# A decoder layer on one core: constant products at the start, the first norms by two token tiles, and a moved turn between two batches

## The chip, the core and the metric

The kernel is one program on one core of a Trainium2 chip. The metric is the time of one execution in microseconds (us), measured on the device. The engines are PE (TensorE: matrix products and transposes), DVE (VectorE), ACT (ScalarE), POOL (GpSimd) and SP (SyncE, which issues most of the transfers here). Each engine works through its own list of instructions in order and waits at an instruction until what it needs has been signalled.

## The reference

Input is x of 4 batches x 512 tokens x 512 features. Three stages, each of them added to x:

```python
x = x + attn(layernorm(x), w_norm, W_in, w_conv, dt_bias, A_log, W_h2i, W_out)
x = x + xattn(layernorm(x), ctx_512, ctx_512)
x = x + ffn(layernorm(x), gate_w, expert_bias, shared_*, experts_*)

# attn: a state-space mixer
xn   = x * rsqrt(mean(x * x) + EPS) * w_norm
proj = xn @ W_in.T                   # z, xi, dt, B, C
xi   = silu(depthwise_conv(xi, width 4))
dt   = softplus(dt + dt_bias);  dA = exp(dt * -exp(A_log))
u    = (dt * mean_over_head(xi))[..., None] * B
h    = dA * h + u  (along the tokens);  y = sum(h * C)
out  = ((y @ W_h2i.T) * silu(z)) @ W_out.T + x_in

# xattn: 32 query heads over 8 key heads of size 16, softmax, keys = values = ctx
# ffn: sigmoid router, 2 of 16 experts per token, and one shared expert
```

The mixer is given layernorm(x), and its own residual adds this input again; so the first stage gives x + layernorm(x) + mixer(layernorm(x)).

## The kernel before

All tokens are held in `res` (128 partitions x 16 token tiles x 512 features). A batch is four token tiles (TB = 4). The mixer of a batch is the generator `ssm(b)`; the attention runs in 32 units (4 batches x 8 key heads) of 8 steps; the router, the shared expert and the blocks of the routed experts follow.

The order of instructions on PE, DVE and ACT is the order in which the Python program writes them (`manual_schedule`); POOL's and SP's lists follow the tile framework. Work that follows a product is not written at once but put on a list, `lag`, with one queue for DVE and one for ACT; `lag.step()` writes out what has become due. The generators yield the estimated PE time of a piece of work, or None where they wait for something on that list.

**The start.** `make_identity` lets POOL write `ident`. The first four token tiles of `res` are loaded by four transfers (L69). `ssm_stats(0)` takes the statistics of the four tiles on DVE (L244, L245) into `smv`, then over all four at once: Sqrt on ACT (L262), three small DVE operations (`square`, L249 to L251), Sqrt on ACT (L266), four small DVE operations (`rest`, L254 to L258). The mixer's own root mean square follows from the variance, so both norms are one scale, `srn`. `ssm_normed(b, j)` writes the normed tile `xn` (L100, on DVE for batch 0 and on POOL later) and on POOL turns the tile of `res` into x + layernorm(x) (L280), with `sr` and `st`. `nega` is -exp(A_log) (L988 on ACT, L989 on DVE).

**The turn.** `ssm_turn(b, j)` transposes `xn` on PE into the PSUM tile `ptx` (L294, four 128x128 transposes) and DVE multiplies it by w_norm into `xnT` (L295); then it calls `ssm_normed(b, j + 2)`, since `xn` has two buffers. PSUM tiles of this kind come from a pool of three. When the four tiles are there, `project` (L311) multiplies `xnT` by pieces of W_in: `pd` (dt), `px`, `pz`, `pb`, `pc`, each of four products, which the trace records as eight.

**Between batch 0 and batch 1.** `ssm(0)` runs alone, without attention beside it. At its end, for each token tile, `po` (L456) is W_out's product, DVE adds it to `res` (L463), takes the statistics for the attention's queries (`part`, L87, L88) and then comes the turn of the tile of batch 1. After the fourth tile `power_q` finishes `rstdq` (L76 on ACT, L77 on DVE), and `norm_queries` lets POOL write the normed queries `qp` (L100). Four pieces of `ssm(1)` are then written, two projections `pd` in two halves each, and after them `queries(0, "q")`: PE transposes `qp` into `ptq` (L532) and ACT copies it to `qTq` (L536).

**The attention's steps.** In each step `maxima` runs two products `pm` (L544) whose maxima DVE takes (L550, into `qp`), `weights` runs `pw` (L561) whose exponentials ACT takes (L565), and `fill(step)` puts in a piece of the next batch's mixer. `pm` and `pw` share a pool of two PSUM tiles. In the first unit there are no `pw` yet. `fill` spends a quota of PE time for each step:

```python
        while owed > 0 or last:
            ...
            if us is not None:
                owed -= us
            elif last:
                lag.step(dve=99.0)
            else:
                return
```

so a piece that waits for the list ends the step's filling, except where the batch's work has to be finished.

## Time and profile before

| | us |
|---|---|
| median of 3 runs | 1420.57 |
| lowest, highest | 1419.97, 1430.86 |
| the profiled execution, its time | 1417.93 |
| its span in the trace | 1415.9 |
| PE busy | 1351.2 (95%) |
| DVE busy | 701.1 (50%) |
| ACT busy | 491.5 (35%) |
| POOL busy | 370.8 (26%) |
| mean granted clock of PE (1 is full) | 0.984 |

A busy PE is not PE at its peak: its clock is granted by a throttle, and the trace gives the granted clock for any stretch. A line of the waits says which engine and line waited for whom, for how many us in total, how often, and the longest. A line of the chain gives start, duration and what ran. A line of the timeline gives start, duration, engine, line, operation, output <- inputs, shapes, number of instructions, and in brackets the idle time before it with what ended it. PEld is PE's loading of weights, which can lie beside its products.

### The profile page before, as it was taken

The page shows a single profiled execution, that of the slowest core. Times are in us where ns is not written, and L with a number is a line of the kernel's source. Part 1 is how long each engine was busy: PE and PEld are TensorE (multiplying, and loading weights), DVE is VectorE, ACT ScalarE, POOL GpSimd, SP SyncE. Part 2 cuts the span into 40 slices and gives each one's busy share as a digit, 9 for nine tenths or more (in the row PEclk, how much of TensorE's full clock was granted, in tenths as well). Part 3 has the DMA queues.
Part 4 walks back from the last instruction along what each step waited for, and adds up shares of the span by engine and source line. Part 5 has one row for each costly group of instructions (what it writes and reads, how often), then busy time and mean ns, then how long its engine had stood idle before and what let it go on. Part 6 is the DMA issues. An engine that isn't in the chain of part 4 may idle for free.

```text
span 1415.9 us, 15833 instructions
## 1 busy us (share of the span) xinstructions
PE 1351.2 (95%) x5776; PEld 538.3 (38%) x5776; DVE 701.1 (50%) x1028; ACT 491.5 (35%) x652; POOL 370.8 (26%) x368
## 2 busy tenths in 40 slices
PE   6999999999999999999999999999999999999894
PEld 3444333333333333333333333333333644444442
DVE  4562656554565645456564446455565653332231
ACT  3220434533544353354434345444443111111110
POOL 4023010302111132111112113212100037776675
PEclk9999999999999999999999999999999899999997
DMA  9200000000000000000000200100000186778764
GB/s 352 31 1 0 0 5 5 4 4 7 4 10 8 4 4 7 6 4 11 6 5 19 66 13 12 31 34 28 29 15 23 52 319 124 138 186 213 205 135 49
DMA packets 61502, 76.84 MB, mean 54 GB/s; under 512 B 22640, under 2 KB 34928, under 8 KB 61168
## 3 DMA queue, kind: packets, MB, share of 16 engines
q1 hardware_dynamic: 45104, 53.24, 11.6%
q0 software_dynamic: 15456, 22.03, 9.0%
q8 instruction: 48, 0.79, 0.2%
q10 hardware_dynamic: 864, 0.55, 0.1%
q14 instruction: 30, 0.25, 0.1%
HBM read 96.76 MB, written 19.92 MB: 82 GB/s over the span
## 4 chain that ended last, share of the span: by engine, by line
PE 86%; DVE 6%; DMA 3%; ACT 2%; issue 1%; POOL 0%; POOLq 0%; SPq 0%; DVEq 0%; ACTq 0%
PE pm L544 18%; PE pgb L1400 9%; PE po L456 8%; PE px L311 8%; PE pz L311 8%; PE pav L571 7%; PE pob L1424 4%; PE pw L561 3%; DVE qp L550 3%; DMA out_x<-y,half_i 2%; PE pd L311 2%; PE pb L311 2%; PE pi L444 2%; PE pc L311 2%; PE pg L688 2%; PE ptq L532 1%
## 5 line engine op out<-in xcount | busy, mean ns | idle before, releaser
L550 DVE TENSOR_REDUCE qp<-pm 128x2 f32<-128x1024 f32 x256 | 313.6, 1225 | 352.3 <-PE pw L561 292.6
L565 ACT ACTIVATE ex<-pw 128x1024 f32<-128x1024 f32 x256 | 262.2, 1024 | 387.7 <-PE pw L561 387.6
L544 PE MATMUL pm<-kt,qTq 16*128 16x512 f32 x1024 | 287.8, 640 | 12.3 <-DVE qp L550 10.8
L561 PE MATMUL pw<-qTm,kt 17*128 17x512 f32 x1024 | 289.5, 641 | 5.1 <-ACT ex L565 4.4
L100 POOL TENSOR_SCALAR qp<-res,mvq,rstdq 128x64 f32<-128x64 f32 x128 | 74.3, 600 | 333.5 <-PE ptm L532 299.4
L1400 PE MATMUL pgb<-ring,xT 128*128 x336 | 153.3, 599 | 2.4 <-DVE xT L1394 2.3
L544 PEld LDWEIGHTS pm<-kt,qTq 16*128 16x128 f32 x1024 | 76.4, 183 | 189.7 <-DVE qp L550 92.3
L1433 POOL DMA_INDIRECT out_x<-y,half_i x84 | 131.5, 1565 | 64.1 <-DMA out_x<-y,half_i 39.3
L571 PE MATMUL pav<-ex,va 128*32 128x512 f32 x1024 | 123.1, 598 | 0.0
L311 PE MATMUL px<-xnT,ssm_large 128*128 128x512 f32 x256 | 121.4, 616 | 0.0
L311 PE MATMUL pz<-xnT,ssm_large 128*128 128x512 f32 x256 | 119.3, 602 | 0.4 <-DVE xc L368 0.3
L456 PE MATMUL po<-ssm_large 128*128 128x512 f32 x256 | 118.5, 599 | 0.0
L590 POOL TENSOR_TENSOR res<-res,o 128x256 f32<-128x256 f32 x32 | 26.7, 833 | 325.8 <-DVE o L586 324.2
L561 PEld LDWEIGHTS pw<-qTm,kt 17*128 17x128 f32 x1024 | 76.8, 183 | 28.8 <-ACT qTm L536 15.0
L1400 PEld LDWEIGHTS pgb<-ring,xT 128*128 128x128 f32 x336 | 61.2, 192 | 64.7 <-issue 61.6
L1424 PE MATMUL pob<-ring,aT 128*128 x168 | 79.1, 593 | 0.5 <-ACT aT L1415 0.5
L368 DVE SCALAR_TENSOR_TENSOR xc<-px,wcv,xc 128x511 f32<-128x511 f32 (+2 forms) x96 | 71.7, 746 | 7.8 <-ACT xc L364 5.6
L311 PEld LDWEIGHTS px<-xnT,ssm_large 128*128 128x128 f32 x256 | 47.2, 194 | 64.8 <-issue 63.1
L1407 DVE TENSOR_TENSOR actb<-pgb,sgb 128x256 f32<-128x256 f32 x42 | 17.8, 424 | 107.3 <-ACT sgb L1405 107.2
L311 PEld LDWEIGHTS pz<-xnT,ssm_large 128*128 128x128 f32 x256 | 45.7, 190 | 63.0 <-issue 59.7
L1429 DVE TENSOR_SCALAR y<-pob,wslot 128x512 f32<-128x512 f32 x42 | 31.5, 751 | 70.6 <-DMA out_x<-y,half_i 44.5
L456 PEld LDWEIGHTS po<-ssm_large 128*128 128x128 f32 x256 | 45.4, 190 | 54.5 <-issue 53.0
(214 smaller groups left out, 1318.4 us busy)
## 6 DMA issues: line engine op xcount, KB each, us to landing
ring<-in_experts SPq DMA_DIRECT2D x42, 1536.0 KB
kt<-in_ctx_t SPq DMA_DIRECT2D x128, 32.0 KB
h_d<-hn SPq DMA_DIRECT2D x16, 256.0 KB
out_x<-res SPq DMA_DIRECT2D x16, 256.0 KB
res<-in_x SPq DMA_DIRECT2D x3, 1024.0 KB
ssm_large<-in_w_in SPq DMA_DIRECT2D x2, 1024.0 KB
ssm_large<-in_w_out SPq DMA_DIRECT2D x1, 2048.0 KB
ssm_large<-in_w_in SPq DMA_DIRECT2D x6, 256.0 KB
```

Source lines behind the costliest of these rows:

```text
L100: eng.tensor_scalar(dst, src, mv[:, j, 0:1], rstd[:, j : j + 1], ALU.subtract, ALU.mult)
L311: nc.tensor.matmul(pm, lhsT=win[:, piece, c, :], rhs=xnT[:, c, :], start=(c == 0), stop=(c == DC - 1),)
L368: nc.vector.scalar_tensor_tensor(xc[:, d:], px[:, : L - d], wcv[:, i, KW - 1 - d : KW - d], xc[:, d:], ALU.mult, ALU.add,)
L456: nc.tensor.matmul(po, lhsT=zg[:, i, ts(j, P)], rhs=wout[:, i, :], start=(i == 0), stop=(i == IC - 1),)
L544: nc.tensor.matmul(ps[:, g - g0, :], lhsT=qT[g * SL : g * SL + HD, ts(j, P)], rhs=kts[i % NQ][g * SL : g * SL + HD, :], start=True, stop=True,
L550: nc.vector.tensor_reduce(qps[i % NQ][:, j, g0 : g0 + 2, HD], ps, AX.X, ALU.max, negate=True)
L561: nc.tensor.matmul(ps[:, g - g0, :], lhsT=kts[i % NQ][rows, ts(c, P)], rhs=qT[rows, :], start=True, stop=True,)
L565: nc.scalar.activation(ex, ps, AF.Exp, scale=1.0 / HD**0.5)
L571: nc.tensor.matmul(pav[ts(g, SL), :], lhsT=vas[b % 2][:, c, v, :], rhs=ex[1 - g // 2][:, g % 2, :], start=(c == 0), stop=(c == TB - 1),)
L1400: weigh(k, nc.tensor.matmul(pg, lhsT=xT[:, c, :], rhs=weight(k, c), start=(c == 0), stop=(c == DC - 1),))
L1424: weigh(k, nc.tensor.matmul(po, lhsT=aT[:, f, :], rhs=weight(k, DC + f), start=(f == 0), stop=(f == FC - 1),))
L1433: add = nc.gpsimd.indirect_dma_start(out=out_halves, out_offset=bass.IndirectOffsetOnAxis(ap=half_i[:, h, k : k + 1], axis=0), in_=y[:, ts ...
```

## The change

1. Behind the constants of the start, PE is given 24 products of `ident` with itself into a PSUM tile `awake` that nobody reads.
2. The statistics of batch 0 go by two halves, tiles 0 and 1 (`lo`) and tiles 2 and 3 (`hi`), written out by hand with the normed tiles between them. `rest` is cut in two: `rest` gives `srn`, and `add` gives `st` and `sr`, for which nothing of the turn waits. For batch 0 `add` and POOL's operation on `res` (now in `ssm_added`) come after all four turns.
3. In batch 0's turn the tiles 1 and 3 are evacuated by ACT, in four operations of 128 columns each (Copy with a scale); tiles 0 and 2 stay with DVE.
4. At the end of `ssm(0)` the query statistics `part(j)` come after the turn of the next batch.
5. `queries(0, "q")` is written after two of the four first pieces of `ssm(1)`, that is between the two `pd`.
6. In the steps before step 4, `fill` steps the list on rather than end the step.

```diff
+    awake = bank("awake", (P, P))
+    for _ in range(24):
+        nc.tensor.matmul(awake, lhsT=ident, rhs=ident, start=True, stop=True)
...
-        def square():
-            nc.vector.reciprocal(r, r)
-            nc.vector.tensor_mul(t, r, r)
-            nc.vector.tensor_mul(t, t, mv[:, :, 1])
-        def rest():
-            nc.vector.reciprocal(rn, rn)
-            nc.vector.tensor_mul(rn, rn, r)
-            nc.vector.tensor_mul(t, r, mv[:, :, 0])
-            nc.vector.tensor_scalar_add(r, r, 1.0)
+        def roots(j):
+            nc.scalar.activation(r[:, j], mv[:, j, 1], AF.Sqrt, bias=eps_ln)
+        def square(j):
+            nc.vector.reciprocal(r[:, j], r[:, j])
+            nc.vector.tensor_mul(t[:, j], r[:, j], r[:, j])
+            nc.vector.tensor_mul(t[:, j], t[:, j], mv[:, j, 1])
+        def roots_n(j):
+            nc.scalar.activation(rn[:, j], t[:, j], AF.Sqrt, bias=eps_rms)
+        def rest(j):
+            nc.vector.reciprocal(rn[:, j], rn[:, j])
+            nc.vector.tensor_mul(rn[:, j], rn[:, j], r[:, j])
+        def add(j):
+            nc.vector.tensor_mul(t[:, j], r[:, j], mv[:, j, 0])
+            nc.vector.tensor_scalar_add(r[:, j], r[:, j], 1.0)
+        if b == 0:
+            return part, roots, square, roots_n, rest, add
...
@@ ssm_normed
         normed(nc.vector if b == 0 else nc.gpsimd, xn, r, mv, ms, j)
+        xns[b, j] = xn
+        if b > 0:
+            ssm_added(b, j)
+    def ssm_added(b, j):
+        mv, ms, r1, mr = ssm_of[b]
+        r = res[:, b * TB + j, :]
         nc.gpsimd.tensor_scalar(
             r, r, r1[:, j : j + 1], mr[:, j : j + 1], ALU.mult, ALU.subtract
         )
-        xns[b, j] = xn
@@ ssm_turn
-        nc.vector.tensor_tensor(
-            xnTs[b][:, :, ts(j, P)], pt,
-            wn.unsqueeze(2).to_broadcast([P, DC, P]), ALU.mult,
-        )
-        ssm_normed(b, j + 2)
+        xT = xnTs[b][:, :, ts(j, P)]
+        if b == 0 and j % 2 == 1:
+            for c in range(DC):
+                nc.scalar.activation(xT[:, c], pt[:, c], AF.Copy, scale=wn[:, c : c + 1])
+        else:
+            nc.vector.tensor_tensor(
+                xT, pt, wn.unsqueeze(2).to_broadcast([P, DC, P]), ALU.mult
+            )
+        if b > 0:
+            ssm_normed(b, j + 2)
@@ ssm, start
             for j in range(TB):
                 ssm_turn(b, j)
+                ssm_normed(b, j + 2)
                 yield TR
+            for j in halves:
+                add_norms(j)
+            for j in range(TB):
+                ssm_added(b, j)
@@ ssm, end
             nc.vector.tensor_add(r, po, r)
-            if b == 0:
-                part(j)
             yield 2 * MM
             if b < B - 1:
                 ssm_turn(b + 1, j)
             else:
                 ffn_turn(0, j, nc.gpsimd)
+            if b == 0:
+                part(j)
             yield TR
@@ the program's order
-    for _, _, fn in ssm_stats(0):
-        fn()
-    for j in range(2):
-        ssm_normed(0, j)
+    part, roots, square, roots_n, rest, add_norms = ssm_stats(0)
+    halves = lo, hi = slice(0, 2), slice(2, TB)
+    part(0); part(1)
+    roots(lo); square(lo); roots_n(lo)
+    part(2); part(3)
+    roots(hi); rest(lo); ssm_normed(0, 0)
+    square(hi); roots_n(hi); ssm_normed(0, 1)
+    rest(hi)
     nc.scalar.activation(nega, nega, AF.Exp)
     nc.vector.tensor_scalar_mul(nega, nega, -1.0)
...
-    for _ in range(4):
+    for n in range(4):
+        if n == 2:
+            qT_of = {0: queries(0, "q")}
         us = next(work)
         done += us or 0.0
         lag.step(dve=99.0)
-    qT_of = {0: queries(0, "q")}
@@ fill
-            elif last:
+            elif last or step < TB:
                 lag.step(dve=99.0)
```

More of the change, by code (lines that the diff above doesn't have):

```diff
@@ L245, in part @@
             nc.vector.bn_aggr(out=mv[:, j, :], in_=st)
-        def square():
-            nc.vector.reciprocal(r, r)
-            nc.vector.tensor_mul(t, r, r)
-            nc.vector.tensor_mul(t, t, mv[:, :, 1])
-        def rest():
-            nc.vector.reciprocal(rn, rn)
-            nc.vector.tensor_mul(rn, rn, r)
-            nc.vector.tensor_mul(t, r, mv[:, :, 0])
-            nc.vector.tensor_scalar_add(r, r, 1.0)
+        def roots(j):
[14 more added lines that the diff above has]
+            return part, roots, square, roots_n, rest, add
+        j = slice(0, TB)
         return (
             *[(ENG.DVE, 0.9, lambda j=j: part(j)) for j in range(TB)],
-            (ENG.Activation, 0.3, lambda: nc.scalar.activation(
-                r, mv[:, :, 1], AF.Sqrt, bias=eps_ln
-            )),
-            (ENG.DVE, 0.6, square),
-            (ENG.Activation, 0.3, lambda: nc.scalar.activation(rn, t, AF.Sqrt, bias=eps_rms)),
-            (ENG.DVE, 0.8, rest),
+            (ENG.Activation, 0.3, lambda: roots(j)),
+            (ENG.DVE, 0.6, lambda: square(j)),
+            (ENG.Activation, 0.3, lambda: roots_n(j)),
+            (ENG.DVE, 0.8, lambda: (rest(j), add(j))),
         )
@@ L981, in route_early @@
         yield from until(lagged(ops + share(0, T1)))
-    for _, _, fn in ssm_stats(0):
-        fn()
-    for j in range(2):
-        ssm_normed(0, j)
+    part, roots, square, roots_n, rest, add_norms = ssm_stats(0)
+    halves = lo, hi = slice(0, 2), slice(2, TB)
+    part(0)
+    part(1)
+    roots(lo)
+    square(lo)
+    roots_n(lo)
+    part(2)
+    part(3)
+    roots(hi)
+    rest(lo)
+    ssm_normed(0, 0)
+    square(hi)
+    roots_n(hi)
+    ssm_normed(0, 1)
+    rest(hi)
     nc.scalar.activation(nega, nega, AF.Exp)
```

## The prediction

> **What bounds the kernel now.** I read the page's busy table and its chain first, then the waits of PE, then the chain and the timeline of the two places that the change touches, and last the stretches with their granted clock.

> ```profile
> PE 1351.2 (95%) x5776; PEld 538.3 (38%) x5776; DVE 701.1 (50%) x1028; ACT 491.5 (35%) x652; POOL 370.8 (26%) x368
> ...
> PE 86%; DVE 6%; DMA 3%; ACT 2%; issue 1%; POOL 0%; POOLq 0%; SPq 0%; DVEq 0%; ACTq 0%
> ```

> PE is the bound nearly everywhere: only its idle time and its slow time can be won, 1415.9 - 1351.2 = 65 us of idle in all, and 28 us of that lie after 1100 us, in the last router and the expert blocks, which this change does not touch. The waits of PE (total, times, longest) say where the rest is:

> ```profile
> PE ptx L294 <- DVE xn L100: 12.0, 2, 11.2
> PE pm L544 <- DVE qp L550: 10.8, 23, 1.5
> ...
> PE pd L311 <- DVE xnT L295: 2.7, 2, 1.9
> ...
> PE pm L544 <- ACT qTq L536: 1.5, 1, 1.5
> ```

> Of the first, 11.2 is the start of the program. Of the second only one wait of 1.34 lies at the start of the attention; 6.8 of the 10.8 fall between 700 and 1000 us. The chain of the start (start, us, what):

> ```profile
> 11.21 1.10 PE ptx L294 x4
> ...
> 12.34 0.69 DVE xnT L295
> 13.03 0.85 DVE xn L100
> ...
> 16.19 0.70 DVE xnT L295
> ...
> 16.93 9.12 PE pd L311 x16
> ```

> The first projection starts at 16.93 and takes 9.12; the same projection of the second batch takes 7.15. So 1.97 us go to a slow PE. The timeline between the batches:

> ```profile
> 136.32 0.66 DVE L295 TENSOR_TENSOR xnT<-ptx,wn 128x512 f32<-128x512 f32 x1
> ...
> 137.04 7.13 PE L311 MATMUL pd<-xnT,ssm_large 128*128 128x512 f32 x16 [1.94 <-DVE xnT L295]
> ...
> 146.08 1.13 PE L544 MATMUL pm<-kt,qTq 16*128 16x512 f32 x4 [1.48 <-ACT qTq L536]
> 147.14 5.40 PE L311 MATMUL px<-xnT,ssm_large 128*128 128x512 f32 x8
> ...
> 154.95 1.13 PE L544 MATMUL pm<-kt,qTq 16*128 16x512 f32 x4 [1.34 <-DVE qp L550]
> ```

> Three waits, and a px that takes 5.33 where eight records at the usual 0.43 are 3.44. The stretches (busy of PE, weight loads, DVE, ACT, POOL; then granted clock, DMA share, GB/s) give the reason:

> ```profile
> 143.97:147.38 3.41, 1.93 (x10) 0.90 (x9) 0.84 (x2) 1.79 (x3) 0.00 (x0) 0.98 0.02 5
> 147.38:150.79 3.41, 3.41 (x5) 1.35 (x5) 1.13 (x1) 0.00 (x0) 0.00 (x0) 0.52 0.00 0
> 1103.02:1106.43 3.41, 3.41 (x18) 3.41 (x18) 0.00 (x0) 1.52 (x3) 0.00 (x0) 0.50 0.34 131
> ```

> After a thin stretch of 3.41 us (transposes, a wait, products of 16 rows) the clock is half for the next one. At the start the column shows 1.00, but weight loads take 0.34 us until 20.85 and 0.19 from 21.17 on, the same pair as around 150.7, so I read that as half clock too. 21.1, 147.38, 150.79 and 1099.6 lie on one grid of 3.41 us. The last line: in a stretch full of transposes and products of 16 columns the clock stays at half.

> **The change, part by part.**

> *The 24 constant products.* They wait for ident, which POOL finishes at 1.72 us; nothing else wants PE before 10 us. In the order of instructions they stand ahead of the first transposes. Each is two records. Their price is bounded by ptab (94 columns, 64 records, 7.5 us busy: 0.118 each at full clock) and by the 16-column pl at half clock (eight in 1.73: 0.22). That is 48 x 0.118 = 5.7 to 48 x 0.22 = 10.6 us, so they end between 7.4 and 12.3. With half clock until about 7.4 (two grid lines after their start) it is some 25 records slow and 23 fast, 5.5 + 2.7, end near 10.

> *Norms by two tiles.* DVE's order is now: statistics 0 and 1, three small operations, statistics 2 and 3, two small, xn0, three small, xn1, two small, nega, xnT0, xn2, xn3, xnT2. From the rows: statistics 1 end at 6.52; Sqrt 0.30 to 6.85; three DVE steps of 0.2 to 7.45; statistics 2 and 3 (0.69, 0.18 and 0.66, 0.18) to 9.16; reciprocal and product to 9.45; xn0 to about 10.05, against 11.1 before, so the first transpose can start at 10.15 instead of 11.21. Then the gain is lost again. ACT runs its second pair of roots at 9.2 and 10.6; the Exp table (1.28, row L988) is loaded only then, to 12.2, Exp of nega ends at 12.4, and DVE's nega operation, which stood at 11.48 before, waits for it at 12.44. Behind it on DVE stand xnT0, xn2, xn3, and PE's third and fourth transposes wait for those. So xnT0 ends at 13.2 (13.03 before), xn2 at 13.75, xn3 at 14.25. xn2 takes 0.55 instead of 0.85, because POOL's operation on res (L280, 2.1 to 2.3) no longer runs beside it. Third and fourth transposes at 1.10 (slow): 13.85 to 16.0.

> *ACT evacuates half.* A slice of 128 columns is not in the trace; it lies between 0.20 (nega, two columns) and 0.37 (aT, 256 columns): 0.28. xnT1 is taken after nega, 12.4 to 13.5, hidden. Of xnT3 only the first slice delays pd: 16.05 + 0.3 = 16.4, against 16.93, where DVE needed the whole 0.70. The three later slices lie under pd's records. The four adds (DVE) and POOL's L301 now follow; the sums are wanted at 112 us by L463, nothing waits. At fast transposes (0.55) pd would start at 15.4.

> *Is PE fast when pd starts?* Between the end of the constant products (about 10) and pd (16.4) PE runs only 16 transposes, 4.2 us at most in 6.3. The stretch 143.97 to 147.38 was busy for 1.93 of 3.41 and the clock fell. So I take it that it falls here as well, and that pd pays the 1.97 again. Start: -0.5 us. The bounds: -0.5 - 1.0 - 1.97 = -3.5 if it stays fast; +0.3 if the constant products stay slow to 12.3 and push everything (ptx0 12.3, xn2 14.6, pd 17.25).
> [...]

> *Statistics after the turn.* xnT of the last tile follows its residual add at once: 135.50 instead of 136.32, pd at 136.2 instead of 137.04: -0.85. What is late next: the queries' statistics end at 137.0 (136.40 before), so the root, the reciprocal and POOL's four operations (0.56 each) end at 140.0 instead of 139.4.

> *Queries between the two pd.* ptq now stands behind the first pd, which ends at 136.2 + 3.44 = 139.65: PE waits about 0.4 for POOL. In return ACT copies qTq at 142.5 (behind Abs, the Exp table, Exp) under the second pd, and pm finds it ready: -1.48 + 0.4 = -1.1. The thin stretch is gone (ptq, pd, pm, px follow each other), so px runs at full clock: 5.33 - 3.44 = -1.9.

> *No step ends early before step 4.* Before, fill returned and left pm 1, 2 and 3 back to back; the third waited 1.34 for a reduction (1.23, two buffers). Now px halves (1.72) stand between them. Followed by hand: reductions of pm1, taps (2.31), plus (1.30), a table load, silu, reductions of pm2 and pm3 end at 157.2 and 158.4 on DVE; PE reaches pm4 at 158.6 and pm5 at 163.1, so neither waits. -1.3. Taps and silu that now stand ahead of the reductions are the cover that could go: one step later on DVE costs what pm4 then waits, up to 1.2. Bounds +1.2 and -1.3.

> *The order after that.* PE's order differs up to the last transposes for batch 2 (some 355 us) and is the same from there on. The amount of work is the same; the waits in that stretch are 0.4 now. I take 0, with the bounds in the rivals.

> Sum: -0.5 - 0.85 - 1.1 - 1.9 - 1.3 = -5.65. Against the profiled execution (span 1415.9, time 1417.93) that is 1412.3. The median of the runs shown, 1420.57, lies 2.64 above it; I forecast for the median: 1414.9.

> **The rivals.**
> *A. PE stays fast into pd.* For: the stretch 133.73 to 137.14 had PE busy for 1.48 of 3.41 and kept its clock. Against: half of that was full products, which the new gap has none of. -3.0 more: 1411.9.
> *B. The drop at 147 is not there to be won.* The clock falls only if the thin piece (144.0 to 147.1) fills one interval of the grid. In timed runs the grid may lie otherwise. Then 1.9 is missing: 1416.8.
> *C. The moved order makes PE wait in the attention.* Place: pm and pw between 160 and 355. For: with the mixture of 700 to 1000 us pm waits 13 times, 6.8 us in all, and a pw waited 1.87 where three table loads stood ahead of its Exp. Against: the amount of filler per step is unchanged. If both appear, +8.7: 1423.6. It decides from 5.65 us of waits on.

> **How the numbers follow.** Forecast 0.57, A 0.17, B 0.18, C 0.08. The likeliest is 1414.9. The range takes in A and its bound below (another 3 us for a drop less in the expert stage, where 1099 to 1113 and 1335 to 1338 run at half clock) and reaches to B and the three runs' spread above: 1408.5 to 1421.5. About 1% (14 us) is what a measurement of this kernel can tell from no change, and all four cases lie within it; beyond it only something not seen here would lead: 0.03 each side, 0.94 within.

> **What would show it.** Right: constant products until about 10 us; nega on DVE near 12.4, right after a table load; pd at about 16.4 with weight loads of 0.34 for its first four microseconds; second pd about 0.85 after the last residual add; no wait of pm on qTq; clock 1.00 around 147. Wrong: weight loads of 0.19 from pd's start (A); half clock between 140 and 160 (B); more than 2 us of waits on qp or ex before 355 (C).

## The result, and the profile after

| | before | after |
|---|---|---|
| median of the timed runs, us | 1424.65 | 1416.24 |
| lowest, highest | 1417.47, 1430.86 | 1410.76, 1421.73 |
| the profiled execution, its time | 1417.93 | 1417.91 |
| its span in the trace | 1415.9 | 1415.8 |

The ratio of after to before is 0.9949 with a 95% interval of 0.9935 to 0.9963, that is 5.3 to 9.3 us less, 7.3 in the middle (the two medians differ by 8.4). The forecast was 1414.9 from a gain of 5.65. The two profiled executions take the same time. That is no contradiction, and b2 below shows why; for this reason the steps are compared between marks inside the traces and not by the spans.

The busy table and the chain of the profile after:

```profile
PE 1361.2 (96%) x5824; PEld 545.1 (39%) x5824; DVE 699.6 (49%) x1033; ACT 493.6 (35%) x662; POOL 369.7 (26%) x368
...
PE 83%; DVE 7%; DMA 5%; issue 2%; ACT 2%; POOL 1%; SPq 0%; POOLq 0%; DVEq 0%; ACTq 0%
```

PE is busy for 10 us more: 7.5 are the constant products, which lie in time that was idle before. PE's waits after (total, times, longest):

```profile
PE pm L574 <- DVE qp L580: 9.2, 22, 1.5
...
PE ptx L314 <- DVE xn L100: 3.2, 3, 2.1
```

One wait on `qp` less (1.6 us less in all), the `xnT` wait between the batches 1.01 where it was 1.94, and no line for `qTq` any more. The start in the timeline:

```profile
1.78 7.48 PE L235 MATMUL awake<-ident 128*128 128x128 f32 x48 [1.78 <-POOL hmean L213]
...
10.87 1.28 ACT L1031 ACT_TABLE_LOAD   x1
...
12.40 0.17 DVE L1032 TENSOR_SCALAR nega<-nega 128x2 f32<-128x2 f32 x1 [1.15 <-ACT nega L1031]
...
13.77 1.94 PE L314 MATMUL ptx<-ident,xn 128*128 128x128 f32 x8 [2.09 <-DVE xn L100]
...
16.17 8.70 PE L341 MATMUL pd<-xnT,ssm_large 128*128 128x512 f32 x16 [0.46 <-ACT xnT L318]
```

DVE waits for a table load before `nega`, everything behind it is late, and `pd` is slow (8.70; the second batch's takes 3.70 + 3.60). The stretches (busy of PE, weight loads, DVE, ACT, POOL; granted clock, DMA share, GB/s):

```profile
9.13:12.54 3.41, 1.44 (x10) 0.84 (x8) 2.08 (x12) 2.25 (x6) 0.00 (x0) 1.00 1.02 402
12.54:15.95 3.41, 1.94 (x8) 1.57 (x8) 2.53 (x8) 1.05 (x5) 0.00 (x0) 0.50 1.01 404
...
142.41:145.82 3.41, 3.41 (x11) 1.43 (x11) 1.88 (x2) 1.32 (x2) 0.63 (x2) 1.00 0.00 0
```

The first line is the gap behind the constant products; the clock falls at its end and stays down until 19.36. The last line is the first `pm` and its `px` in the second batch, now at full clock. That place in the timeline:

```profile
134.93 3.70 PE L341 MATMUL pd<-xnT,ssm_large 128*128 128x512 f32 x8 [1.01 <-DVE xnT L320]
138.47 0.60 PE L562 MATMUL ptq<-ident,qp 128*128 128x128 f32 x4
138.91 3.60 PE L341 MATMUL pd<-xnT,ssm_large 128*128 128x512 f32 x8
142.44 1.13 PE L574 MATMUL pm<-kt,qTq 16*128 16x512 f32 x4
143.49 3.70 PE L341 MATMUL px<-xnT,ssm_large 128*128 128x512 f32 x8
147.12 1.13 PE L574 MATMUL pm<-kt,qTq 16*128 16x512 f32 x4
```

Of the stalls of before, the wait on `qTq` and the slow `px` are gone, and the wait before `pd` is 0.93 shorter. The wait of the third `pm` is gone as well, but the row that shows its price comes with j3.

### The profile page after: what moved, and what is told of

The parts are those of the page before. It is cut to its first block, busy times and chain, and to the rows that moved or that the text cites. A ratio compares the mean times of both kernels' runs of the same rounds, so it can differ in the third digit from the quotient of the medians.

```text
span 1415.8 us, 15947 instructions
## 1 busy us (share of the span) xinstructions
PE 1361.2 (96%) x5824; PEld 545.1 (39%) x5824; DVE 699.6 (49%) x1033; ACT 493.6 (35%) x662; POOL 369.7 (26%) x368
## 3 DMA queue, kind: packets, MB, share of 16 engines
HBM read 96.76 MB, written 19.92 MB: 82 GB/s over the span
## 4 chain that ended last, share of the span: by engine, by line
PE 83%; DVE 7%; DMA 5%; issue 2%; ACT 2%; POOL 1%; SPq 0%; POOLq 0%; DVEq 0%; ACTq 0%
PE pm L574 18%; PE po L486 8%; PE pz L341 8%; PE px L341 8%; PE pav L601 8%; PE pgb L1444 7%; PE pob L1468 3%; DMA out_x<-y,half_i 3%; PE pw L591 3%; DVE qp L580 3%; PE pd L341 2%; PE pb L341 2%; PE pi L474 2%; PE pc L341 2%; PE pg L718 2%
## 5 line engine op out<-in xcount | busy, mean ns | idle before, releaser
L100 POOL TENSOR_SCALAR qp<-res,mvq,rstdq 128x64 f32<-128x64 f32 x128 | 73.9, 596 | 335.6 <-PE ptm L562 301.2
L1426 POOL DMA_INDIRECT res<-h_d,row_i x42 | 45.6, 1085 | 74.2 <-DVE half_i L1288 41.9
```

Source lines behind the costliest of these rows:

```text
L100: eng.tensor_scalar(dst, src, mv[:, j, 0:1], rstd[:, j : j + 1], ALU.subtract, ALU.mult)
```

## The experiments

| run | median, us | before beside it | ratio | 95% interval |
|---|---|---|---|---|
| a1_no_awake | 1417.32 | 1422.67 | 0.9961 | 0.9940 to 0.9983 |
| a2_bridge | 1414.03 | 1422.67 | 0.9929 | 0.9904 to 0.9955 |
| a3_nega_late | 1411.71 | 1422.67 | 0.9903 | 0.9870 to 0.9937 |
| a4_old_start | 1418.35 | 1422.67 | 0.9964 | 0.9944 to 0.9984 |
| j1_stats_first | 1414.62 | 1422.42 | 0.9935 | 0.9912 to 0.9958 |
| j2_queries_late | 1418.12 | 1422.42 | 0.9972 | 0.9953 to 0.9992 |
| j3_steps_end | 1415.59 | 1422.42 | 0.9937 | 0.9910 to 0.9964 |
| k1_fill_thin | 1425.72 | 1422.42 | 1.0019 | 0.9994 to 1.0044 |
| a5_bridge_nega | 1411.89 | 1425.48 | 0.9917 | 0.9891 to 0.9943 |
| p2_bridge_thin | 1410.51 | 1425.48 | 0.9895 | 0.9871 to 0.9919 |
| j4_dve_turns | 1415.09 | 1425.48 | 0.9937 | 0.9914 to 0.9960 |
| b2_before_again | 1420.04 (one run) | | | |

The intervals are some 0.005 wide, 7 us, and most single parts are 0.5 to 3 us. So the times alone separate few of these runs; the traces do, since the same mark of PE's order can be read to 0.1 us. (The median of a3, for one, is a little below that of a5, which contains its edit and starts the first `px` 2.9 us earlier.) At the start a trace also has its own shift of some tenths: the first transposes start at 9.74 to 10.19 in the traces with the new start.

### The start: a1, a2, a3, j4

**a1, without the constant products.**

```diff
-    awake = bank("awake", (P, P))
-    for _ in range(24):
-        nc.tensor.matmul(awake, lhsT=ident, rhs=ident, start=True, stop=True)
```

> The changed kernel without the 24 constant products. Theory (the clock has fallen again before the first projection, so the products buy nothing): the first transposes run at 1.1 us a tile instead of 0.55, but DVE waits for nega until 12.4 anyway; pd starts at 16.2 to 16.6 and its first four weight loads or so take 0.34; the time is that of the changed kernel within 1 us, ratio to the kernel before 0.995. Rival (on the average over runs the products do carry the clock into pd): 2 us slower than the changed kernel, ratio 0.9965, with a profile that looks like that of the kernel before at 17 to 26 us.

Measured: `pd` starts at 15.94, takes 8.33, and the first `px` starts at 24.10 (24.71 with the products). The ratio, 0.9961, lies nearer to the rival's 0.9965 than to the theory's 0.995, but its interval holds both. One trace does not decide it either, since the grid of the clock lies elsewhere in each execution (its first line at 0.1 to 3.3 us in the fourteen traces) and the end of the slow time with it. All traces together do: without constant products `pd` takes 8.33 to 9.40, in the mean 8.87 (before, b2, a1, a4, k1); with the 24 products and the gap behind them 8.59 to 9.08, in the mean 8.86 (after, a3, j1 to j4). So the products as they stand buy nothing in `pd`.

**a2, more products in the gaps between the transposes** (`keep(n)` issues n of them, all into a tile of another pool).

```diff
+    keep(24)
...
+                if j == 0:
+                    keep(3)
...
+                keep((1, 8, 0, 2)[j])
```

> The changed kernel with 14 more constant products, set where PE is idle between the first ones and pd: 3 ahead of the first turn, 1 behind it, 8 behind the second, 2 behind the fourth (all write a PSUM tile of the attention's pool, which nobody reads). Theory (it is the thin gap that takes the clock back): granted clock 1.00 from 12 to 20 us, last two transposes 0.55 each, pd starts at about 15.3 with weight loads of 0.19, px starts at 22.4 instead of 24.7, 2.3 us less than the changed kernel, ratio to before 0.9935. Rival (products of 128 columns and transposes are too light to hold the clock, or the grid decides): the clock falls all the same, and the products ahead of the third turn take 0.44 each and delay it by up to 1.5 us: 0 to 1.5 us slower than the changed kernel.

Measured, in PE's timeline:

```profile
15.19 7.13 PE L350 MATMUL pd<-xnT,ssm_large 128*128 128x512 f32 x16
22.16 3.17 PE L350 MATMUL px<-xnT,ssm_large 128*128 128x512 f32 x7
```

The transposes of the last two tiles take 1.11 where they took 1.94, `pd` 7.13 where it took 8.70, and `px` comes 2.55 us earlier. Beside the products in the gaps only the place of the grid differs, and that is not the reason: in the six traces with the open gap (after, a3, j1 to j4) the clock falls at 11.8 to 14.4 us wherever the grid lies, and in the three with filled gaps (a2, a5, p2) it does not fall there and `pd` takes 7.13 each time. The thinnest interval of the gap is busy for 2.74 of 3.41 us here (8.03 to 11.44), where it was 1.44. So the gap behind the 24 products is what loses their effect.

**a3, DVE's nega operation behind the turns.**

```diff
     nc.scalar.activation(nega, nega, AF.Exp)
-    nc.vector.tensor_scalar_mul(nega, nega, -1.0)
...
             for j in range(TB):
                 ssm_added(b, j)
+            nc.vector.tensor_scalar_mul(nega, nega, -1.0)
```

> The changed kernel with DVE's multiplication of nega moved behind the turns and the adds of batch 0 (ACT's Exp stays where it is). Theory (DVE's wait for the Exp table is what takes back the gain of the two-tile norms): xnT0 at 11.3 instead of 12.48, xn2 and xn3 by 13.1, third transposes at 12.6 instead of 13.8, pd at 15.1 instead of 16.17; 1.1 us less than the changed kernel. Rival (ACT is next late: xnT1 behind the table load, or slow transposes set the pace): pd at 15.8 to 16.2, less than 0.4 us gained.

Measured: the first `xnT` starts at 11.02 (12.48), the third and fourth transposes at 12.31 (13.77), `pd` at 14.71 (16.17): 1.46 us earlier, 0.4 more than expected. 0.15 of this is the trace's own shift. Counted from the first transposes, the third follow after 2.35, where they follow after 3.32 to 3.67 in the five other traces with the open gap. So the cost of the order around `nega`, 1.0 to 1.3 us at the third transposes, is shown. `pd` is slow still (9.07), so `px` starts at 23.62, 1.09 earlier. That the order is worth this much at `px` is not shown, since the grid alone moves it by more: j1 has the start of the changed kernel, but its clock falls only at 14.37, behind the transposes, and `pd` starts at 14.81 and `px` at 23.24.

**j4, DVE evacuates all four turns.**

```diff
-        if b == 0 and j % 2 == 1:
-            for c in range(DC):
-                nc.scalar.activation(xT[:, c], pt[:, c], AF.Copy, scale=wn[:, c : c + 1])
-        else:
-            nc.vector.tensor_tensor(
...
+        nc.vector.tensor_tensor(
...
```

> The changed kernel with one part undone: DVE evacuates all four of the first turns, ACT none. Theory: xnT of the second tile stands on DVE ahead of the fourth norm, and xnT of the fourth tile takes 0.70 in one piece where ACT's first slice took 0.28; pd starts at about 16.7 instead of 16.17, +0.5, and the first px by as much later; the ratio is not told from 0.9949. Rival: DVE is idle in the gaps anyway, and ACT's slices (1.12 in all, of which pd waits for one) save nothing: pd within 0.2 of 16.17. Second rival: the third and fourth transposes are pushed as well, +0.7 or more on top: pd after 17.2.

Measured: `pd` starts at 16.52, and its first transposes at 9.94 where the changed kernel's start at 10.11. From first transpose to `pd` that is 6.58 against 6.06: ACT's share is worth 0.52, as expected.

### The join of the two batches: a4, j1, j2, j3, k1

To compare these runs I take one mark, the ninth `ptq` (near 380), counted from the last `ptx` before the second batch's `pd`. Behind that `ptq` the order on PE is the same in all of them. Where the clock falls to half shortly before the mark, `ptq` is 0.95 later; the changed kernel has 246.63 with such a fall and 245.68 (a2, which differs at the start only) without one before the mark. The kernel before has 250.43 without: 4.75 more than a2.

**a4, the kernel before with parts 4, 5 and 6 of the change** (as in the diff of the change, nothing of the start).

> The kernel before with only the edits between the batches: statistics after the turn, queries between the two pd, steps 0 to 3 not ended early. Start as before: pd at 16.93, 9.1 us long. Theory (nearly all of the gain is between the batches): pd of batch 1 follows the last residual add by 0.7 instead of 1.6 us, no wait of pm on qTq, no half clock near 147, no wait of pm on qp before 170; 5.1 us less than the kernel before, ratio 0.9964, that is 0.5 to 1 us slower than the changed kernel. Rival (the start gives 2 us or more in the average run): ratio 0.9975 or more.

Measured: ratio 0.9964 as expected; `pd` of the first batch starts at 17.12 and takes 9.40, the join goes as in the changed kernel.

**j1, the statistics ahead of the turn.**

```diff
+            if b == 0:
+                part(j)
             if b < B - 1:
                 ssm_turn(b + 1, j)
...
-            if b == 0:
-                part(j)
```

> The changed kernel with one part undone: in the second batch's tiles the statistics stand ahead of the turn again. Theory: xnT of the last tile waits for them on DVE, so the second batch's first projection starts about 0.85 us later after the last residual add than in the changed kernel (134.93 - 133.59 = 1.34 there, about 2.2 here) with a wait of about 1.9 instead of 1.01; the statistics end earlier by as much, and everything behind the projection is the same but for that 0.85. Rival: the queries, which need the statistics, then come earlier and PE, which did not wait for them in the changed kernel, gains nothing or wins part of it back: less than 0.4 lost by the first pm. In the whole time 0.85 is 0.0006 of the ratio and will not be told from the changed kernel's 0.9949; the trace decides.

Measured: `pd` waits 1.94 again; the mark is at 246.60 without a fall, 0.92 more than 245.68.

**j2, the queries behind both `pd`.**

```diff
-    for n in range(4):
-        if n == 2:
-            qT_of = {0: queries(0, "q")}
+    for _ in range(4):
...
+    qT_of = {0: queries(0, "q")}
```

> The changed kernel with one part undone: the query transposes stand behind both projections again, not between them. Theory: the first pm waits about 1.4 us for the copy qTq (none in the changed kernel), and the transposes, that wait and the 16-row products form a thin stretch again; if it fills an interval of the 3.41 us grid, px behind it runs at half clock for one interval (1.7 us lost). So +1.4 without and +3.1 with the drop, a ratio between 0.9959 and 0.9971 against 0.9949. Rival: what kept the clock up in the changed kernel was not the order but where the grid lay; then the wait is back and the clock stays at 1.00 here too, +1.4 only. Second rival: the wait is not back, as the copy has nothing ahead of it on ACT: 0.

Measured, in PE's timeline and in the stretches:

```profile
143.68 1.13 PE L574 MATMUL pm<-kt,qTq 16*128 16x512 f32 x4 [1.48 <-ACT qTq L566]
144.74 5.40 PE L341 MATMUL px<-xnT,ssm_large 128*128 128x512 f32 x8
```

```profile
142.01:145.42 3.41, 1.94 (x8) 0.74 (x7) 1.29 (x2) 1.58 (x3) 0.77 (x2) 1.00 0.00 0
145.42:148.82 3.40, 3.40 (x6) 1.34 (x5) 0.69 (x1) 0.00 (x0) 0.00 (x0) 0.50 0.00 0
```

The wait is back, and behind the thin stretch the clock falls. The mark is at 249.88 with a fall, 3.25 more than 246.63. The forecast had 1.1 + 1.9 for this.

**j3, a step may end early.**

```diff
-            elif last or step < TB:
+            elif last:
```

> The changed kernel with one part undone: a step may end early again when its filler returns, also before step 4. Theory: pm 1, 2 and 3 stand back to back, the third waits about 1.3 us for a reduction, and the next pm come earlier in order; +1.3 by 165 us, ratio 0.9958. Rival: the wait only moves, since the px halves that stood between the pm are used up later: 0 by the last transposes of the batch at about 350 us. Third: the order from there on brings its own waits, either sign up to 2 us.

Measured, in PE's timeline:

```profile
147.20 1.14 PE L574 MATMUL pm<-kt,qTq 16*128 16x512 f32 x8
149.69 1.13 PE L574 MATMUL pm<-kt,qTq 16*128 16x512 f32 x4 [1.34 <-DVE qp L580]
```

The wait of 1.34 is back, but the mark is at 247.21 with a fall: only 0.58 more. The first line tells where most of the rest is. The products of two successive steps, eight records, take 1.14 us when they stand back to back; the changed kernel pays 1.13 for each four (147.12 and the rows after it). So the separation by `px` halves takes away the wait and gives up about 1.0 of overlap, and 1.34 - 1.0 leaves 0.3. Smaller waits are 0.15 more: up to the mark PE waits for 4.72 us in j3 and for 3.23 in the changed kernel, 1.49 and not 1.34 apart. The last 0.1 is not accounted for. What lets eight records take the time of four is not shown.

The three parts undone one by one cost 0.92 + 3.25 + 0.58 = 4.75, the whole difference at the mark.

**k1, the kernel before with six constant products in the wait on `qTq`.**

```diff
+    thin = p_av.tile([P, L], F32, tag="av", name="thin")
+    for _ in range(6):
+        nc.tensor.matmul(thin[:, :P], lhsT=ident, rhs=ident, start=True, stop=True)
```

> The kernel before with one addition: six constant products of 128 columns between the query transposes and the first pm of the attention, where PE waited 1.48 us for the copy qTq and the clock was half in the next 3.41 us. Theory (a thin stretch takes the clock): the products last about 12 x 0.12 = 1.4 us, fill the wait, and px behind it runs at full clock, 3.44 instead of 5.33: -1.9 in the trace, ratio 0.9987. Rival 1: the thin stretch is not the cause; px still takes 5.3, ratio 1.000 (to +0.3 us if the products overshoot the wait). Rival 2: the drop only moves on to the next thin place within some ten us, and the -1.9 is lost again by 165 us.

Measured, in PE's timeline and in the stretches:

```profile
144.16 1.50 PE L1006 MATMUL thin<-ident 128*128 128x128 f32 x12
...
146.86 3.70 PE L311 MATMUL px<-xnT,ssm_large 128*128 128x512 f32 x8
```

```profile
149.87:153.28 3.41, 2.07 (x12) 0.61 (x12) 1.59 (x2) 2.65 (x4) 0.00 (x0) 1.00 0.00 0
153.28:156.70 3.42, 3.42 (x7) 0.95 (x4) 3.35 (x5) 2.12 (x4) 0.00 (x0) 0.50 0.00 0
```

At the filled place the theory holds: `px` takes 3.70 (5.40 in the kernel before). But the second rival comes true beside it: the next thin place, three `pm` with the wait of 1.34 between them, now lay in one interval of the grid (149.87 to 153.28, PE busy for 2.07 us), and the clock was half for 6.8 us from 153.28 on. In j3 a line of the grid lies among the same three `pm` (147.20 to 150.82), near 149.4 by an estimate from its slow `px` at 381.51 (5.31 us for 3.70), and nothing fell. Nothing is won in time (1.0019). This is one trace, and the place of the grid may decide here too. The changed kernel removes both thin places, not one.

### Where the lead goes, and a better version: b2, a5, p2

**b2, the kernel before unchanged, for a second profile.**

> The kernel before once more, unchanged, for a second profile. Theory: its first profile is one of its quickest executions because it kept full clock near 385 and lost only 3.4 us near 630; where the grid of 3.41 us lies otherwise, the same work is at half clock there for 6.8 us each, as in most profiles of the changed kernel, and the execution is 3 to 5 us longer (1420 to 1424). Rival: the kernel before keeps its clock near 385 whatever the grid, because its order there differs; then this profile shows 1.00 there again, and the drop at 377 to 385 is a cost of the change.

Measured, the stretches around 385 in the first profile of before, then in the second:

```profile
382.78:386.19 3.41, 2.32 (x10) 1.18 (x11) 2.27 (x4) 2.73 (x5) 1.97 (x4) 1.00 0.05 10
386.19:389.60 3.41, 3.41 (x15) 1.26 (x13) 0.56 (x1) 2.14 (x4) 0.00 (x0) 1.00 0.05 10
```

```profile
382.37:385.78 3.41, 2.15 (x10) 1.15 (x11) 2.41 (x4) 2.72 (x5) 1.79 (x4) 1.00 0.02 4
385.78:389.20 3.42, 3.42 (x5) 1.38 (x5) 0.73 (x1) 1.77 (x4) 0.00 (x0) 0.50 0.06 16
```

The same instructions, with the grid 0.4 us earlier: in the first profile the clock stays, in the second it falls. So the theory holds in kind; the fall lasted 3.4 us, not 6.8 as expected, and 6.8 near 630 (3.4 in the first). The execution took 1420.04. Over the first profile of before the changed kernel leads by 4.98 us near 380, 2.7 near 410, 1.45 near 660, -0.2 near 1036. Over the second it leads by 4.74, 4.17, 4.39 and 2.80 at these marks. What looked like a lead lost behind the change is a first profile of before that lost little to the clock.

**a5, a2 and a3 together,** with three products behind the second turn instead of eight.

> The changed kernel with both repairs of its start: constant products also in the gaps between the transposes (3 + 1 + 3 + 2 of them), and DVE's nega operation behind the last turn. Theory: the two add. The transposes of the third tile start at about 12.3 (as with nega late alone) and run fast, so pd starts about 13.9 to 14.2 (16.17 in the changed kernel, 15.19 with the products alone, 14.71 with nega late alone), has weight loads of 0.19 from the start and takes 7.1, and px starts at 21.0 to 21.3 (24.71). That is -3.5 us, a ratio of about 0.9925 if the changed kernel's is 0.9949. Rival: with nega late the gaps are so short that the products overshoot and push the transposes; then pd starts no earlier than 14.7 and px at 21.8. Second rival: the weights of pd (loaded by DMA) land after 14.2 and pd waits for them.

Measured, in PE's timeline:

```profile
13.79 7.13 PE L351 MATMUL pd<-xnT,ssm_large 128*128 128x512 f32 x16
20.76 4.46 PE L351 MATMUL px<-xnT,ssm_large 128*128 128x512 f32 x10
```

`px` starts 3.95 us earlier than in the changed kernel, a little more than expected, and the lead is still 4.0 near 1036. No fall before 373.

**p2, a5 and constant products ahead of two `pm`** where the next `pw` waited 1.86 and 2.53 us in the changed kernel (unit 7 and unit 15, step 6).

```diff
         ps = p_sc.tile([P, 2, L], F32, tag="sc", name=f"pm{i}_{step}")
+        for _ in range({(7, 6): 7, (15, 6): 10}.get((i, step), 0)):
+            nc.tensor.matmul(ps[:, 0, :P], lhsT=ident, rhs=ident, start=True, stop=True)
```

> The kernel with both repairs of the start, and constant products ahead of two more pm products, where the next pw waits for an exponential (1.87 us near 378, 2.53 us near 622 in the changed kernel) and the clock fell to half for 6.8 us in nearly every profile: 7 and 10 of them, 1.65 and 2.4 us long, inside the waits. Theory (thin stretches take the clock): no half clock near 380 and 625, 3.4 us saved at each place, so -6.8 against the start repairs alone: ratio 0.988 if theirs is 0.9925. Rival 1: the drop moves on to the next thin place, as it did when the wait of 1.48 at the kernel before was filled (half clock at 153 in place of 147): 0 to -3.4. Rival 2: the products push pm and the waits grow: +0.5 to +1.

Measured, in PE's timeline, first of the changed kernel and then of p2:

```profile
377.94 2.08 PE L591 MATMUL pw<-qTm,kt 17*128 17x512 f32 x4 [1.86 <-ACT ex L595]
...
380.85 5.46 PE L341 MATMUL px<-xnT,ssm_large 128*128 128x512 f32 x8
```

```profile
371.14 1.72 PE L584 MATMUL pm<-ident 128*128 128x128 f32 x14
...
374.23 1.13 PE L603 MATMUL pw<-qTm,kt 17*128 17x512 f32 x4 [0.31 <-ACT ex L607]
...
375.79 3.60 PE L351 MATMUL px<-xnT,ssm_large 128*128 128x512 f32 x8
```

The wait of the `pw` shrinks from 1.86 to 0.31, and `px` behind it takes 3.60 (5.46 in the changed kernel); the later wait of 2.53 is gone, and in this profile there is no half clock between the first `pd` and 961. Between the traces of a5 and p2 the lead is 2.9 us near 410 and 5.85 near 660 (6.8 was expected), and stays 5.85 to 1036. In the timed runs the median is 1.4 us lower and the intervals of the two ratios overlap: that p2 beats a5 is shown in the traces and not in the times. Against the kernel before it is the quickest version run, 0.9895.

## Why the prediction was right, step by step

| step | forecast, us | measured, us | read from |
|---|---|---|---|
| start, to the second batch's last `ptx` | -0.5 | -1.2 (134.50 to 133.32); -1.0 against b2 | marks |
| statistics after the turn | -0.85 | -0.92 | j1 |
| queries between the `pd`, clock at `px` | -1.1 - 1.9 | -3.25 | j2 |
| no step ended early | -1.3 | -0.58 | j3 |
| sum | -5.65 | -5.95 | |
| timed runs | | -7.3 (-5.3 to -9.3) | ratio |

**The start.** Forecast: the constant products end near 10 (9.26), `nega` on DVE at 12.44 (12.40), the last transposes slow from 13.85 (13.77), `pd` at 16.4 (16.17) and slow. All of it came, a1 and a2 show why the products do not reach `pd`, a3 that the order around `nega` holds the transposes. The bound below, -3.5 against the kernel before if PE stays fast, is what a2 reached: its first `px` starts at 22.16, 3.73 before the 25.89 of the kernel before. a5, which moves `nega` as well, has 5.13. The gain was sized too small, -0.5 for -1.2. 0.4 of these 0.7 is no gain of the change: I carried over the whole loss of 1.97 of before, and here `pd` takes 8.70, 0.4 less than 9.12, because the end of the half clock (19.36) lies where the grid puts it; over all traces the two are equal (a1). That the gain is larger than 0.5 holds beyond this pair: in four traces with the old start (before, b2, a4, k1) the last `ptx` stands at 134.22 to 134.97, in the mean 134.50, and in four with the new one (after, j1, j2, j3) at 131.85 to 133.40, in the mean 132.90. One reason in the working stays open: in the kernel before the third tile's norm took 0.92 (12.95) and the fourth's 0.53 (14.39), both with POOL's operation on `res` beside them (11.17 to 13.48, 13.54 to 19.92), so POOL alone does not explain why the third took longer. In the changed kernel, without it, the two take 0.99 together.

**The statistics** went as forecast.

**The queries.** The mechanism was right. Two sizes were off in opposite directions: PE does not wait 0.4 for POOL, because POOL starts at 136.34, its four operations (0.56 each) end near 138.6, and `ptq`, which starts at 138.47, goes tile by tile and needs the last of them only with its last transpose; and the gain at `px` is 1.7 (5.32 in j2 to 3.63 here, from its start to the next `pm`), not 1.9.

**No step ends early.** This term was sized too large: -1.3 forecast, -0.58 measured. I followed DVE's reductions and found no new wait, which was right, and counted PE's products by their length alone; that two steps' products overlap when they stand back to back was in the trace of before (eight records in 1.14 us at 152.47, four in 1.13 at 154.95) and I did not look.

**The order after that** was taken as 0. At the mark near 380 it is 0, since the three parts add up to the whole. Behind it the two profiles of before drift 3.2 us apart between 380 and 660 on the same instructions. Whether the 1.4 us between the sum of the steps and the middle of the timed runs is more than noise is not shown; the interval holds both.

**The sum.** That it comes within 0.3 us of the forecast is in part luck: the start gave 0.7 more than forecast and the last part 0.7 less.

**The rivals.** A (PE stays fast into `pd`) did not come; it needs the products in the gaps (a2). B (the drop at 147 is not there to be won) did not come: both profiles of before and j2 show the drop, with the grid at three different places, and in j2 the thin piece does not even fill its interval (142.01 to 145.42 ends with 0.68 us of `px`); and none of the ten traces with the queries between the two `pd` has half clock between 25 and 160 us. C (waits from the moved order) did not come: between 145 and 355 PE waits for less than 0.5 us in all. The median lies 1.3 above the forecast, although the gain was larger, because the base was different: the runs beside it put the kernel before at 1424.65, not 1420.57. The ratio that was forecast, 1414.9 / 1420.57 = 0.9960, lies inside the measured interval, near its upper end.

## What to carry to other kernels

Work that is put in to keep PE's clock up has to reach the work that matters: 24 products followed by a thin gap bought nothing in `pd`, 14 more inside the gaps brought it from 8.70 to 7.13 us. When one thin place is filled, look at the next one: in k1 it took over, in p2 none did. Before an order is changed to spread small products out, look whether they overlap where they are; and before two traces are compared by their spans, look at a second profile of the same kernel.

## What the runs showed of the hardware

**What counts as thin.** Not the busy share alone: behind the stretch at 382.37 with PE busy for 2.15 of 3.41 us the clock fell, and behind the one of the prediction with 1.48 (133.73; 1.49 of 3.41 when cut on the grid) it did not. The first holds products of 16 and 17 rows, transposes and 0.6 us of full products, the second 0.9 us of full products beside its transposes. Full products alone do not separate the two kinds: in a1 the clock fell behind a stretch with 1.0 us of them, busy for 2.11 in all (373.36). Nor does a stretch have to be idle: in the intervals before 640 us behind which the clock fell, PE was busy for 0.98 to 2.20 of 3.41 us. Where the boundary lies was not settled.

**Between the runs.** What follows the first `ptab`, near 1120 us, took 288.3 to 296.3 us in the fourteen traces, whose kernels do the same work there. A part of 1 us at the start cannot be read from one pair of spans.
